# Two more pauses of the router with each scatter of rows to their slots

## The chip, the cores and the metric

The kernel runs on one core of a Trainium2 chip. The metric is the device time of one execution in microseconds: 3101.64 us in the median of three runs (3100.33 to 3101.95). TensorE does the matrix products, VectorE and ScalarE the arithmetic along rows, GpSimd causal selects, some arithmetic and indirect transfers, and SyncE issues most of the other transfers.

## The reference, cut to what matters

The model has two layers over x of shape 2 x 2048 x 256. The first layer normalises x and adds causal attention (16 heads of 16) and a mixture of experts:

```python
xn = _layernorm(x, axis=-1)
x = x + _L0_attn_ref(xn, ...) + _L0_ffn_ref(xn, ...)
```

In `_L0_ffn_ref` a second normalisation is followed by a gate: of eight experts (256 to 1024 to 256) each token takes the two with the largest logits, weighted by a softmax of the two. The second layer is a selective state space with a short convolution, and a ternary product beside it; nothing in this case touches it.

```python
logits = xn @ gate_w_moe + gate_b_moe
tw, ti = jax.lax.top_k(logits, K)
h = jax.nn.gelu(jnp.einsum('bsd,edf->besf', xn, w1) + b1[None, :, None, :], approximate=False)
```

The reference runs every expert on every token. The kernel sorts the tokens by expert instead, and that is where the change lies.

## The kernel before, in words

There are 4096 tokens, kept as 32 blocks of 128 rows. The kernel has four phases: a first one that normalises, projects q, k and v and computes the gate's logits; `attention`; `experts`; and `mix_and_state_space`. The first writes the normalised rows to DRAM (`n2_d`) and the parts of q and k too (`qk_d`).

Attention goes through 16 stages, each a batch and a pair of heads, numbered 0 to 15 here. Two generators work through them. `first` computes for every query the maximum over its keys (`maxima`, lines 652 to 678: scores on TensorE, reduced on VectorE). `second` follows 22 units behind (`LAG`) and does the attention proper (`attend`): scores again with the maximum subtracted (line 750), the exponential on ScalarE (line 758), and in the four key blocks that cross the diagonal of each group of 512 queries a causal select on GpSimd (line 763). A stage has 40 units in each generator; in `attend` they are four groups of 4, 8, 12 and 16 key blocks, whose last four each have a select, so a stage has 16 selects in groups of four. The value matmuls (line 705) wait for the exponential and, on the diagonal, for the select. They are put into the code some units later than their scores.

The q and k of a stage are loaded by `stacked` (line 554): 16 transfers of 128 KB on SyncE's queue, eight for q and eight for k. `first` calls it for stage s+1 when it begins stage s. There are three buffers for each, so the loads of stage 3 wait until stage 0's last scores are done, and so on.

Between these units the router runs (`route`). The loop in `attention` takes three units, then advances the router by one step, up to its next `yield`; there are 434 such steps. The router's first 25 steps compute on VectorE which experts each token takes and which slot (a row of `x_d` in DRAM) each of its two copies gets. Then, for block n of 32, it issues the load of block n+1 (`load`, line 973, on SyncE's queue, 128 KB) and two scatters (line 984): indirect transfers issued by GpSimd that write the block's 128 rows to their slots in `x_d`, once for each of the two experts. After each scatter it advances `finish_route`, which computes the experts' weights and row numbers, and yields; after the second there is one more yield. So a block takes three steps, and block n's first scatter is in step 26+3n. The tile `rows` has two buffers: row block n+2 can be loaded when both scatters of block n have landed. The scatters all write `x_d`, and each waits until the one before it has landed.

Attention is not in a manual schedule (that begins in the last phase). Tile lays down the order of each engine's queue when the program is built: an engine that is free takes, of the instructions whose inputs and buffers are held to be ready by then, the one that was written first. So instructions may be issued long before their place in the code when their engine is free. On the chip each queue runs in that fixed order.

`experts` reads `x_d` in tiles of 256 slots, after attention has ended.

Of the kernel before, what the change touches and what calls it, by code (L numbers as in the profile page):

```python
# [101 lines left out]
def tile_model(ctx: ExitStack, tc: tile.TileContext, t, out):  # L102
# [55 lines left out]
    with ExitStack() as c0:  # L158
# [9 lines left out]
        with tc.tile_pool(name="vs", bufs=1) as vsp, tc.tile_pool(name="qk", bufs=3) as qk:  # L168
# [6 lines left out]
            with tc.tile_pool(name="pa", bufs=2) as pa, tc.tile_pool(  # L175
# [154 lines left out]
                v,  # L330
                xa,
                lambda gp, ps: route(tc, row, ones, lg, n2_d, x_d, keep, stage, gp, ps, routes),
            )

# [515 lines left out]
def route(tc, row, ones, lg, n2_d, x_d, keep, stage, gp, ps_m, out):  # L850
# [120 lines left out]
    def load(n):  # L971
        rows = stage.tile([P, D], F32, tag="rows", name=f"rows_{n}")
        nc.sync.dma_start(rows, n2_d[:, n, :])
        coming.append(rows)
# [4 lines left out]
    for n in range(NT):  # L979
        if n + 1 < NT:  # L980
            load(n + 1)
        rows = coming.pop(0)
        for i in range(TOP):
            nc.gpsimd.indirect_dma_start(
                out=x_d[:, :],
                out_offset=bass.IndirectOffsetOnAxis(ap=slots[:, i, n : n + 1], axis=0),
                in_=rows,
                in_offset=None,
            )
            next(rest, None)  # L990
            yield
        next(rest, None)
        yield
    for _ in rest:
# [946 lines left out]
```

## Time and profile before

| | |
|---|---|
| median of three runs | 3101.64 us |
| the profiled execution | 3103.07 us |
| its span | 3101.4 us |
| granted TensorE clock, mean | 0.894 |
| the router's scatters | 238.4 to 539.1 us, 64 of them |
| attention's first causal select | 210.2 us |
| first load of an expert's weights | 1277.8 us |
| scatter, busy on GpSimd | 0.97 us in the median |
| scatter, issue to landing | 2.4 us in the median, 8.6 at most |

All durations come from one profiled execution, taken by the hardware profiler. An entry such as "PE pv L705 <- POOL p L763" reads: TensorE, about to run line 705, which writes the tile pv, stood idle until GpSimd had done line 763, which writes p. In the order of time a line gives the start and the length in us, the engine, the line of the code, the operation, and in brackets the idle time before it and what ended it; lines in a row of the same kind are merged with their count. SPq is SyncE's queue of transfers, and its lines show when transfers are issued, not when they land. The granted clock is a share of TensorE's full clock.

### The profile page before, as it was taken

The numbers are of one execution on the slowest core, as the hardware profiler recorded it, in microseconds if no ns is written. First come the engines' busy times: TensorE is split into PE (matmuls) and PEld (weight loads), VectorE is DVE, ScalarE is ACT, GpSimd is POOL, SyncE is SP. The second block draws the span as 40 slices with busy tenths as digits, with TensorE's granted clock in tenths as the row PEclk, the third lists the DMA queues.
The fourth block names the chain that finished last, engine by engine and source line by source line (L and its number), as shares of the span: only waits on it lengthen the run. The fifth ranks groups of instructions, "written<-read, shape, count | busy, mean of one in ns | idle before, by whom it ended". The sixth has DMA issues, their size and how long they took to land. (4 is left out here: it accounts for less than half of the span.)

```text
span 3101.4 us, 40083 instructions
## 1 busy us (share of the span) xinstructions
PE 2693.9 (87%) x15085; PEld 1472.6 (47%) x15085; DVE 2047.8 (66%) x2566; ACT 1577.7 (51%) x2522; POOL 1185.5 (38%) x933
## 2 busy tenths in 40 slices
PE   6887888999999999799999997687879889898867
PEld 4543433445444444587888886332323232332213
DVE  7576766887888888233111101368999898999996
ACT  3424555666566666422322222457666566666542
POOL 4313223000111011111112111267797887878775
PEclk9978988999999999899999999787888877788758
DMA  8843214112332210433445554124443634445350
GB/s 292 217 123 79 57 50 86 28 29 42 56 42 28 29 28 8 156 135 137 146 153 185 197 188 107 58 67 96 112 118 72 149 82 110 108 97 118 83 112 14
DMA packets 120086, 309.55 MB, mean 100 GB/s; under 512 B 27936, under 2 KB 70304, under 8 KB 102352
## 3 DMA queue, kind: packets, MB, share of 16 engines
q1 hardware_dynamic: 99968, 206.53, 28.2%
q0 software_dynamic: 18576, 99.24, 9.5%
q8 instruction: 122, 2.00, 0.3%
q10 hardware_dynamic: 1344, 1.16, 0.1%
q14 instruction: 76, 0.62, 0.1%
HBM read 228.48 MB, written 78.38 MB: 99 GB/s over the span
## 5 line engine op out<-in xcount | busy, mean ns | idle before, releaser
L758 ACT ACTIVATE p<-s 128x1024 f32<-128x1024 f32 (+3 forms) x640 | 563.3, 900 | 386.6 <-PE s L750 365.9
L665 DVE TENSOR_REDUCE best<-m 128x2 f32<-128x1024 f32 (+3 forms) x640 | 669.6, 1062 | 111.7 <-PE m L652 100.8
L1829 POOL TENSOR_TENSOR hh<-hh,cc 128x2048 f32<-128x2048 f32 x128 | 579.4, 4526 | 10.6 <-POOL carry L1828 0.4
L1817 DVE TENSOR_TENSOR_SCAN hh<-decay,uh 128x2048 f32<-128x2048 f32 x128 | 565.8, 4420 | 24.3 <-ACT decay L1703 10.5
L705 PE MATMUL pv<-p,v 128*17 128x256 f32 (+1 forms) x4608 | 384.2, 380 | 52.3 <-POOL p L763 49.5
L763 POOL TENSOR_SCALAR_AFFINE_SELECT p<-p 128x256 f32<-128x256 f32 x256 | 103.4, 408 | 787.0 <-ACT p L758 785.9
L1703 ACT ACTIVATE decay<-dd,a_neg 128x511 f32<-128x511 f32 x512 | 332.3, 711 | 54.7 <-DVE hh L1817 54.3
L1118 ACT ACTIVATE hT<-h,b1s 128x256 f32<-128x256 f32 x296 | 137.8, 473 | 385.9 <-PE h L1111 385.8
L1727 DVE TENSOR_TENSOR uh<-dd,bb 128x2048 f32<-128x2048 f32 x128 | 293.6, 2294 | 56.8 <-PE bb L1714 48.2
L1132 DVE TENSOR_TENSOR yt<-o,b 128x512 f32<-128x512 f32 x37 | 25.6, 691 | 436.8 <-PE o L1124 436.8
L750 PE MATMUL s<-q,k 64*128 64x512 f32 (+3 forms) x1280 | 287.9, 437 | 22.5 <-DVE best L665 17.5
L652 PE MATMUL m<-k,q 64*128 64x512 f32 (+3 forms) x1280 | 281.9, 427 | 18.0 <-DVE best L665 8.9
L1111 PE MATMUL h<-xT,w 128*128 128x256 f32 x1184 | 276.2, 387 | 19.9 <-ACT hT L1118 8.3
L1714 PE MATMUL bb<-xp_sb,w_dt 16*128 16x512 f32 x256 | 184.8, 808 | 103.8 <-DVE uh L1727 103.8
L1124 PE MATMUL o<-w,hT 128*128 128x256 f32 x1184 | 261.8, 379 | 0.0
L1074 POOL DMA_INDIRECT w<-in_w,wrow x74 | 71.2, 962 | 478.1 <-PE h L1111 255.3
L1111 PEld LDWEIGHTS h<-xT,w 128*128 128x128 f32 x1184 | 227.0, 194 | 55.0 <-ACT hT L1118 8.7
L750 PE MATMUL s<-tops,onesr 64*128 64x512 f32 (+3 forms) x1280 | 248.2, 371 | 0.0
L1124 PEld LDWEIGHTS o<-w,hT 128*128 128x128 f32 x1184 | 225.1, 190 | 30.5
L1744 PE MATMUL y<-hh,sel 128*32 128x512 f32 x1024 | 180.9, 787 | 57.5 <-POOL hh L1829 57.0
L705 PEld LDWEIGHTS pv<-p,v 128*17 128x17 f32 x4608 | 107.9, 97 | 235.5 <-issue 113.6
L750 PEld LDWEIGHTS s<-q,k 64*128 64x128 f32 x1280 | 127.0, 188 | 168.4 <-DVE best L665 55.8
(334 smaller groups left out, 3463.3 us busy)
## 6 DMA issues: line engine op xcount, KB each, us to landing
dd<-dd_d SPq DMA_DIRECT2D x120, 512.0 KB, 6.9
q<-qk_d SPq DMA_DIRECT2D x128, 128.0 KB, 4.1
k<-qk_d SPq DMA_DIRECT2D x128, 128.0 KB, 7.5
x_d<-zero SPq DMA_DIRECT2D x6, 1664.0 KB
xg<-x_d SPq DMA_DIRECT2D x37, 256.0 KB, 6.6
y_d<-yt SPq DMA_DIRECT2D x37, 256.0 KB, 2.2
qk_d<-qp SPq DMA_DIRECT2D x16, 512.0 KB, 3.7
qk_d<-kp SPq DMA_DIRECT2D x16, 512.0 KB, 3.3
```

The source lines that it names most:

```text
L652: nc.tensor.matmul(ps[:, h, 0:n], lhsT=qT[hs, qs], rhs=kT[hs, c * CH : c * CH + n], start=True, stop=True, tile_position=(HP * h, 0),)
L665: nc.vector.tensor_reduce(best[:, i, :, c], ps[:, :, 0:n], AX.X, ALU.max)
L705: nc.tensor.matmul(pv[r0 : r0 + HS + 1, lo - f * HC : HC], lhsT=v[:, b * TPB + kb, 2 * pr + h, :], rhs=pt[:, h, lo:hi], start=(kb == 0), s ...
L750: nc.tensor.matmul(ps[:, h, off:CH], lhsT=(kT[hs, kb * P : (kb + 1) * P], onesr[hs, :])[i], rhs=(qT[hs, j * CH + off : (j + 1) * CH], tp[h ...
L758: nc.scalar.activation(pt[:, :, off:CH], ps[:, :, off:CH], AF.Exp, scale=float(HS) ** -0.5)
L1111: nc.tensor.matmul(ph, lhsT=w1[:, k * DF + f * P : k * DF + (f + 1) * P], rhs=xT[:, k, :], start=(k == 0), stop=(k == 1),)
L1124: nc.tensor.matmul(po[:, h, :], lhsT=hT[:, f, h * P : (h + 1) * P], rhs=w2[:, f * D : (f + 1) * D], start=(f == 0), stop=(f == NF - 1),)
L1703: nc.scalar.activation(decay[G % 2][:, q, 1:], of[at]["dd", n // 4][:, 0, q, 1:], AF.Exp, scale=a_neg[:, q, n : n + 1],)
L1714: nc.tensor.matmul(bb[:, 0, :], lhsT=w_dt[DR + DS :, (n % 4) * P : (n % 4 + 1) * P], rhs=of[at]["xp"][DR + DS :, :], start=True, stop=True,)
L1727: nc.vector.tensor_tensor(uh, of[at]["dd", n // 4][:, 1], of[at]["bb", n].to_broadcast(full), ALU.mult)
L1817: nc.vector.tensor_tensor_scan(hh.rearrange("p q c -> p (q c)"), decay[G % 2].rearrange("p q c -> p (q c)"), uh.rearrange("p q c -> p (q c)"),
L1829: nc.gpsimd.tensor_tensor(hh, hh, m_["cc", g].to_broadcast(full), ALU.mult)
```

## The change

After each scatter, before the yield that was there, the router yields twice more.

```diff
                 in_offset=None,
             )
             next(rest, None)
+            yield
+            yield
             yield
         next(rest, None)
         yield
```

No instruction is added or removed. A block now takes seven of the router's steps instead of three: its first scatter is in step 26+7n, the second three steps later. The loads of the following blocks move along with it, and so do the first five advances of `finish_route`. The last scatter, which was in step 120, is in step 246 of 434.

## The prediction

> **What bounds the kernel now.** I read the page's engine totals first, then the busy time in stretches cut at attention's stages, then the list of waits between 230 and 560 us, where the scatters run, and last the order of time on SyncE's queue, on GpSimd and on TensorE around one of the long waits.
>
> ```profile
> PE 2693.9 (87%) x15085; PEld 1472.6 (47%) x15085; DVE 2047.8 (66%) x2566; ACT 1577.7 (51%) x2522; POOL 1185.5 (38%) x933
> ```
>
> TensorE is the busiest engine, but the share is an average. The change touches attention alone, so the next view is cut there: each line is one stage (a batch and a pair of heads), from its first causal select (line 763) to the next stage's. The last two numbers but one are the granted clock and the DMA share.
>
> ```profile
> 301.32:365.16 63.84, 59.77 (x526) 28.05 (x526) 48.07 (x80) 38.44 (x57) 15.21 (x25) 0.92 0.15 38
> 365.16:446.30 81.14, 63.71 (x555) 29.23 (x554) 54.76 (x91) 41.79 (x63) 20.05 (x30) 0.91 0.27 61
> 446.30:516.28 69.98, 63.10 (x540) 29.46 (x540) 50.89 (x81) 39.72 (x60) 23.01 (x33) 0.91 0.32 77
> 516.28:587.35 71.07, 58.82 (x526) 27.80 (x526) 50.01 (x83) 38.26 (x57) 11.27 (x22) 0.90 0.26 49
> 587.35:649.48 62.13, 59.41 (x545) 27.87 (x546) 52.01 (x85) 40.09 (x61) 6.46 (x17) 1.00 0.23 35
> 649.48:710.20 60.72, 58.73 (x546) 27.98 (x544) 52.01 (x85) 39.78 (x61) 6.45 (x16) 1.00 0.25 38
> ```
>
> These are stages 1 to 6. Stages 5 and 6 hold no scatter: TensorE is busy for 97% of them, and their mean, 61.4 us, is what a stage costs undisturbed. Stages 2, 3 and 4, with scatters, take 19.7, 8.6 and 9.7 us more. The waits say why; columns are us in total, times, longest:
>
> ```profile
> PE pv L705 <- POOL p L763: 49.0, 15, 10.9
> POOL x_d L984 <- DMA x_d<-rows,slots: 125.9, 53, 7.9
> ```
>
> A scatter may not start before the one before it has landed, and that wait stands in GpSimd's queue ahead of the causal selects; TensorE's value matmuls wait for the selects. One such place in full, start and length in us, GpSimd and then TensorE:
>
> ```profile
> 370.42 0.98 POOL L984 DMA_INDIRECT x_d<-rows,slots  x1 [1.80 <-DMA x_d<-rows,slots]
> 371.43 0.41 POOL L763 TENSOR_SCALAR_AFFINE_SELECT p<-p 128x256 f32<-128x256 f32 x1
> 373.39 0.99 POOL L984 DMA_INDIRECT x_d<-rows,slots  x1 [1.55 <-DMA x_d<-rows,slots]
> 378.49 0.97 POOL L984 DMA_INDIRECT x_d<-rows,slots  x1 [4.11 <-DMA x_d<-rows,slots]
> 387.17 0.97 POOL L984 DMA_INDIRECT x_d<-rows,slots  x1 [7.71 <-DMA x_d<-rows,slots]
> 389.86 0.97 POOL L984 DMA_INDIRECT x_d<-rows,slots  x1 [1.73 <-DMA x_d<-rows,slots]
> 390.85 1.12 POOL L763 TENSOR_SCALAR_AFFINE_SELECT p<-p 128x256 f32<-128x256 f32 x3
> 391.31 1.91 PE L705 MATMUL pv<-p,v 128*17 128x256 f32 x16 [10.91 <-POOL p L763]
> ```
>
> An undisturbed chain of scatters has one every 2.7 us (387.17 to 389.86). Here one takes 8.7 us, because a stage's sixteen q and k loads go out on SyncE's queue at that moment (a line with a count spans all its issues):
>
> ```profile
> 300.12 57.14 SPq L973 DMA_DIRECT2D rows<-n_d  x5
> 362.38 0.79 SPq L554 DMA_DIRECT2D q<-qk_d  x2
> 366.64 0.34 SPq L973 DMA_DIRECT2D rows<-n_d  x1
> 367.02 0.42 SPq L554 DMA_DIRECT2D q<-qk_d  x1
> 373.18 0.34 SPq L973 DMA_DIRECT2D rows<-n_d  x1
> 373.56 2.28 SPq L554 DMA_DIRECT2D q<-qk_d  x5
> 375.89 5.16 SPq L554 DMA_DIRECT2D k<-qk_d  x8
> 386.96 39.27 SPq L973 DMA_DIRECT2D rows<-n_d  x4
> ```
>
> The same happens four times. From the last uninterrupted run of q loads to the scatter that gets going again it is 12.4, 13.6, 12.9 and 13.8 us (287.92 to 300.31, 373.56 to 387.17, 467.73 to 480.60, 521.66 to 535.42), 13.2 in the mean.
>
> **What the change does to the order.** Two more yields add no instruction. They move each scatter, and the load issued with it, later in the code: block n goes from router step 26+3n to 26+7n, of 434 steps. The order on the engines does not simply follow: 19 scatters are issued by the end of stage 0 (301 us), where the code has reached 6, since GpSimd is idle and takes what is ready. The code's order decides only between things that are ready together, and it does so on SyncE's queue: the loads of stage 4's q and k are written at step 73. Rows 15 and 16 (steps 68, 71) are written before them and lie between them in the trace; row 17 (step 74) and later come after. With the change rows 8 and up are written after step 73, rows 12 and up after stage 5's loads (step 100), and so on. So from stage 4's loads on, each block of sixteen goes out undivided, and the rows wait behind it. Stage 3's loads show that form already: sixteen undivided, then five rows (300.12, the only gap of that kind) before stage 4's loads become ready. I therefore expect: nothing different up to about 362 us; then rows 15 to 19, 20 to 24, 25 to 29, 30 and 31 in the gaps behind the loads of stages 4, 5, 6 and 7, and the last scatter at about 620 us in place of 538 (three stages of 68 us after 365, and 38 us into the fourth, as in stage 1, plus four times 2.7).
>
> **The cost, part by part.** The issues themselves are the same 64 scatters of 0.97 us and 32 row loads; GpSimd is busy 6.5 of 61 us in a stage without scatters, so they lie beside other work, as 9 of them do in stage 1 (63.84 us, 2.4 over the plain 61.4, of which a wait of 1.5 after a collision is part). The later end costs nothing: x_d is read by the experts after 1277 us, some 650 us later. The rest of the router's arithmetic (finish_route) is issued at 223 us already, ahead of its place in the code, and is needed at 1277. A row load that now stands behind sixteen others delays only scatters, and in stage 1's form it is issued some 40 us before its scatter. So the cost lies in the collisions.
>
> At the loads of stage 4 the tail of the chain is rows 13 and 14 (scatters at 361.45, 364.15, 366.84, 370.42 in the trace). Undivided loads start where the first does now, 362.38, when stage 1's last scores free the buffer. 13.2 us on is 375.6, so the last scatter goes at 375.6 where it now goes at 370.42. The select behind it (371.43) and the value matmul behind that (371.89, which already waits 0.28 us for it) are late by 5.2 us. What follows a stall: stages 2, 3 and 4 lose 19.7+8.6+9.7 = 38.0 us, and their TensorE stalls of over 1.2 us sum to 28.3 (10.91, 2.37; 1.74, 1.65, 2.13; 1.22, 8.29): 9.7 us more over seven stalls, 1.4 each. So a boundary costs about 6.6 us. The bounds for it: 0, if the tail has passed, and 12.3, the largest stall plus 1.4. I take 6.6, since it is stage 4's own scatters that it is worked out from.
>
> After the change there are four such boundaries (into stages 2, 3, 4 and 5): 26.4 us. The other stalls of these stages (10.91, 8.29 and the small ones among divided loads) go. Before, stages 2 to 6 lose 19.7+8.6+9.7+0.7-0.7 = 38.0. The sum is -11.6 us. Against the profiled execution, 3103.07 us (span 3101.4 and 1.67 around it), that gives 3091.5; that execution lies 1.4 us over the median of the runs, so the median forecast is 3090.
>
> One rule speaks against a gain. The trace shows a lower granted clock after each stall: 0.73 in 310 to 320 us and 0.79 in 540 to 550, 1.00 in the stretches after. The Trainium skill, page "TensorE: Matmul & The Clock Gate", section Terms, prices throttled time at its length times one minus the clock ratio. The records show half clock in pieces of 3.4 to 13.7 us, mostly 6.8, so by that page a boundary is estimated at 5.2+3.4 = 8.6, four of them at 34.4, and the change at -3.6 us, within what can be measured. The trace disagrees in stage 4, where 9.5 us of stalls cost 9.7 us in all: a stage is not bound by the clock alone.
>
> **The rivals.** (1) Slower: the undivided loads cost the worst row at each boundary. Rows for it: 10.91 at 391.31, and 7.39 plus 1.53 at 301.79, where the loads were undivided too. Four times 12.3 is 49.2 against 38.0: +11, 3113. It decides from 9.5 us a boundary on. Against it: at 390 four scatters stood ahead of the select, and the new tail has one behind the last three selects. (2) The tail misses the loads: if only four rows fit into a gap, or the selects of the next stage come first, stages 3 to 5 cost some 0.7 each; 6.6+2.1 against 38.0 is -29, 3072. Against it: stage 1's gap held five. (3) The pauses do spread the scatters, one in three steps (61.4 us is 26.7 steps, so 6.9 us), longer than 2.7: every stall goes, also those of stage 0, where 62.9 us from the first scatter on hold 28 of 40 units of a stage, 43 us. That is 19.9+2.4+38.0 = -60, 3041. Against it: the 19 scatters in stage 0. (4) The order stays and nothing changes: 3101.6.
>
> **How the numbers follow.** Chances: forecast 0.42, (1) 0.28, (2) 0.13, (3) 0.08, (4) 0.09. Faster or slower begins at 0.2%, 6.2 us, about what a measurement of this kernel can tell from no change. Faster: 0.31 of the forecast, all of (2) and (3): 0.52. The same: 0.11 of the forecast, 0.05 of (1), 0.08 of (4): 0.24. Slower: 0.23 of (1) and 0.01 of (4): 0.24. The forecast's own range is 3080 to 3102. The whole range, 3064 to 3116, leaves out (3) and the far ends of (1) and (2).
>
> **What would show it.** Equal traces up to 362 us; sixteen undivided loads from about 362; five rows behind them; the last scatter near 620 us; TensorE waits of some 5 us at each of four boundaries; stages 2 to 5 at about 68 us and stage 6 at 61. Wrong would be: scatters 7 us apart from the start (rival 3), waits of 8 us or more at the boundaries (1), none (2), or a different stage 0.

## The result, and the profile after

The changed kernel takes 3116.84 us in the median of six runs (3115.22 to 3119.7), the kernel before 3098.47 us in the same comparison. The ratio is 1.0059, with a 95% interval from 1.0049 to 1.007: slower by 0.6%, where the forecast was faster by 0.4% (3090), and just above the end of its range (3116). The profiled execution after took 3118.85 us, with a span of 3117.1 against 3101.4, so 15.7 us more.

The first line of the page, engine totals with their shares and instruction counts, after:

```profile
PE 2707.8 (87%) x15085; PEld 1477.9 (47%) x15085; DVE 2048.8 (66%) x2566; ACT 1578.5 (51%) x2522; POOL 1185.6 (38%) x933
```

The work is the same and the times of VectorE, ScalarE and GpSimd agree within 1.0 us, but the same 15085 matmuls kept TensorE busy for 13.9 us longer (2693.9 before). So TensorE hardly waited longer: it worked more slowly. The stretches by stage say where; these are stages 1 to 6 after, each from its first causal select to the next stage's (the granted clock and the DMA share are the third- and second-last numbers):

```profile
302.83:363.83 61.00, 57.45 (x526) 27.21 (x527) 48.01 (x80) 38.42 (x57) 15.21 (x26) 0.96 0.17 40
363.83:444.60 80.77, 65.91 (x549) 30.05 (x548) 54.76 (x87) 41.41 (x62) 16.21 (x27) 0.87 0.31 57
444.60:519.50 74.90, 65.82 (x546) 30.57 (x546) 52.86 (x86) 40.47 (x61) 16.20 (x27) 0.89 0.26 55
519.50:591.02 71.52, 62.27 (x528) 28.92 (x528) 48.38 (x80) 38.26 (x57) 16.25 (x26) 0.84 0.26 52
591.02:664.00 72.98, 63.69 (x545) 29.13 (x546) 52.05 (x85) 40.29 (x61) 12.29 (x23) 0.91 0.26 46
664.00:724.69 60.69, 58.73 (x546) 27.98 (x544) 52.03 (x85) 39.78 (x61) 6.45 (x16) 1.00 0.26 37
```

Stages 2 to 6 take 360.86 us in sum and took 345.04 before: 15.8 more, which is the whole difference of the spans (what lies ahead of them is 1.3 us shorter, what follows 1.3 longer). Over the plain 61.4 us they lose 53.9 us, where the forecast had 26.4 and the kernel before 38.0. All of it lies in stages 2 to 5, which is where the forecast put its four boundaries.

SyncE's queue after (start, length from the first to the last issue, count):

```profile
361.04 3.62 SPq L554 DMA_DIRECT2D q<-qk_d  x8
364.70 7.03 SPq L554 DMA_DIRECT2D k<-qk_d  x8
372.48 66.29 SPq L973 DMA_DIRECT2D rows<-n_d  x5
```

From the loads of stage 4 on, sixteen q and k loads go out undivided with five rows behind them, as the prediction had it. The last scatter is at 648.56 us. So the order came out as forecast; what it costs did not. GpSimd and TensorE at the first of the four boundaries:

```profile
360.12 0.98 POOL L984 DMA_INDIRECT x_d<-rows,slots  x1 [0.32 <-issue]
362.82 0.98 POOL L984 DMA_INDIRECT x_d<-rows,slots  x1 [0.68 <-DMA x_d<-rows,slots]
370.10 0.98 POOL L984 DMA_INDIRECT x_d<-rows,slots  x1 [5.86 <-DMA x_d<-rows,slots]
371.11 0.77 POOL L763 TENSOR_SCALAR_AFFINE_SELECT p<-p 128x256 f32<-128x256 f32 x2
371.58 1.06 PE L705 MATMUL pv<-p,v 128*17 128x128 f32 x8 [4.58 <-POOL p L763]
379.08 0.98 POOL L984 DMA_INDIRECT x_d<-rows,slots  x1 [7.20 <-DMA x_d<-rows,slots]
380.09 0.41 POOL L763 TENSOR_SCALAR_AFFINE_SELECT p<-p 128x256 f32<-128x256 f32 x1
380.56 0.62 PE L705 MATMUL pv<-p,v 128*17 128x128 f32 x4 [4.24 <-POOL p L763]
```

The loads catch two scatters, not one: the one issued at 362.82 lands after 7.0 us and the next, at 370.10, after 8.7 (the scatters behind them go 7.3 and 9.0 us later, against 2.7 in an undisturbed chain). Each has a select behind it, and TensorE stalls twice, 4.58 and 4.24 us, with 4.7 us of work between. The last scatter of the tail goes 18.0 us after the first load (361.04 to 379.08). At the other three boundaries the stalls are 3.33 and 3.44 us; 3.79, 4.14 and 2.79; 3.48 and 3.58: in sum 33.4 us for four boundaries, 8.3 each.

Yet all waits of this kind together have hardly changed. The list of waits from 230 to 760 us (total, times, longest), after; before, the same entry was 49.0, 15 and 10.9:

```profile
PE pv L705 <- POOL p L763: 51.7, 17, 7.0
```

What changed is their lengths: five stalls of over 2.5 us before (3.60, 6.06, 7.39, 10.91, 8.29), twelve after, of which one is over 5. And with it the clock. Stretches around the first boundary after (length, TensorE's busy time, ..., granted clock, DMA share, GB/s):

```profile
367.00:371.60 4.60, 0.02 (x4) 0.02 (x5) 1.59 (x5) 0.38 (x1) 1.47 (x3) 0.69 1.01 155
371.60:376.30 4.70, 4.70 (x21) 1.46 (x21) 2.14 (x2) 2.05 (x5) 0.28 (x1) 0.50 1.00 127
376.30:380.60 4.30, 0.06 (x4) 0.05 (x4) 0.32 (x1) 0.00 (x0) 1.40 (x2) 0.50 0.53 95
380.60:389.40 8.80, 8.80 (x48) 4.24 (x50) 4.22 (x10) 3.44 (x4) 0.00 (x0) 0.51 0.10 30
389.40:398.00 8.60, 8.55 (x80) 4.05 (x72) 6.69 (x9) 4.49 (x6) 1.63 (x4) 1.00 0.00 0
```

and around the one long stall of the kernel before, at about the same place:

```profile
380.40:391.30 10.90, 0.01 (x2) 0.00 (x0) 1.68 (x2) 0.38 (x1) 2.39 (x4) 0.65 0.62 107
391.30:397.40 6.10, 6.08 (x36) 2.32 (x36) 1.66 (x2) 1.41 (x2) 1.07 (x3) 0.50 0.13 43
397.40:404.00 6.60, 6.32 (x61) 2.88 (x60) 5.32 (x9) 4.22 (x5) 0.00 (x0) 1.00 0.01 2
```

After, TensorE idles 8.8 us, and in between and afterwards works 13.5 us at half the clock. Before, it idles longer, 10.9 us, but only 6.1 us of work runs at half the clock: most of the slow clock falls into the stall itself, where there is nothing to slow down.

To add this up I cut 230 to 760 us of each kernel into stretches of one microsecond and summed TensorE's idle time, and the time that it worked at half the clock (where the clock changes within a stretch, the part at half clock, at most the busy time); the work in it takes twice its time, so half of it is lost.

| kernel | idle, us | working at half clock, us | idle + half of that | span |
|---|---|---|---|---|
| before | 65.8 | 47.5 | 89.5 | 3101.4 |
| after | 66.7 | 74.9 | 104.1 | 3117.1 |

The idle time accounts for 0.9 us of the difference and the clock for 13.7, together 14.6 of 15.7.

### The profile page after: what moved, and what is told of

It reads as the page before. It is cut to its first block, busy times and chain, and to the rows that moved or that the text cites. A ratio compares the mean times of both kernels' runs of the same rounds, so it can differ in the third digit from the quotient of the medians.

```text
span 3117.1 us, 40079 instructions
## 1 busy us (share of the span) xinstructions
PE 2707.8 (87%) x15085; PEld 1477.9 (47%) x15085; DVE 2048.8 (66%) x2566; ACT 1578.5 (51%) x2522; POOL 1185.6 (38%) x933
## 5 line engine op out<-in xcount | busy, mean ns | idle before, releaser
L1819 DVE TENSOR_TENSOR_SCAN hh<-decay,uh 128x2048 f32<-128x2048 f32 x128 | 565.8, 4420 | 24.4 <-ACT decay L1705 10.5
L652 PE MATMUL m<-k,q 64*128 64x512 f32 (+3 forms) x1280 | 284.3, 430 | 17.1 <-DVE best L665 8.6
```

What stands on the lines that cost most here:

```text
L652: nc.tensor.matmul(ps[:, h, 0:n], lhsT=qT[hs, qs], rhs=kT[hs, c * CH : c * CH + n], start=True, stop=True, tile_position=(HP * h, 0),)
L1819: nc.vector.tensor_tensor_scan(hh.rearrange("p q c -> p (q c)"), decay[G % 2].rearrange("p q c -> p (q c)"), uh.rearrange("p q c -> p (q c)"),
```

## The experiments

The theory, from this reading: the loss lies where a chain of scatters, each waiting for the one before, is still unfinished when the next stage's loads go out; the landings then take 7 to 9 us instead of 2.4 and the selects behind them are late. Rivals: the loads alone cost it, whatever the scatters do; the divided order of before is cheap in itself; the scatters cost by their number. The first five kernels are variants of the changed kernel and are compared with the kernel before by their times; the last three are variants of the fourth and are read from their profiles.

**No chain at the later boundaries.** Row loads and scatters of blocks 15 to 31 are left out, so those rows of `x_d` are not written.

```diff
-    for n in range(NT):
-        if n + 1 < NT:
+    for n in range(15):
+        if n + 1 < 15:
```

> The changed kernel without the row loads and scatters of blocks 15 to 31, so that x_d lacks them; all else is kept, and the queues' order is the changed kernel's up to the boundary into stage 2. Theory (the loss sits at the boundaries, where undivided q and k loads hold up the tail of the scatters): stage 2 keeps the first boundary's two stalls, 4.6 and 4.2 us, and takes about 75 us, stages 3, 4 and 5 fall from 74.9, 71.5 and 73.0 to about 61.4, and the time to about 3076. Rival (the undivided loads disturb TensorE by themselves, scatters or not, by traffic or by the clock): stages 3 to 5 stay above 68 and the time above 3100.

It took 3073.41 us, 0.9903 of before (0.9884 to 0.9922). Stages 2 to 4:

```profile
364.27:439.18 74.91, 64.65 (x545) 29.80 (x546) 52.23 (x85) 40.30 (x61) 8.39 (x18) 0.89 0.21 34
439.18:499.89 60.71, 58.74 (x546) 27.96 (x544) 52.07 (x85) 39.88 (x61) 6.51 (x17) 1.00 0.25 37
499.89:559.42 59.53, 56.93 (x536) 27.08 (x534) 51.12 (x85) 39.81 (x60) 6.51 (x16) 1.00 0.27 36
```

Without scatters the undivided loads of the following stages cost nothing: 60.7 and 59.5 us at full clock. The one boundary that is left still has its two stalls, 4.42 us (ending at 371.88) and 3.64 (380.26), and stage 2 takes 74.9 us, 13.5 over the plain 61.4. Stage times and total came out as the theory had them (about 75, about 61.4, about 3076).

**No loads.** From stage 4 on the buffers of earlier stages are used again, so the q and k of stages 4 to 15 are wrong and 192 loads are missing.

```diff
-                    stacks[s + 1] = stacked(nc, qk, qk_d, s + 1)
+                    stacks[s + 1] = stacks[s - 2] if s > 2 else stacked(nc, qk, qk_d, s + 1)
```

> The changed kernel without the q and k loads of stages 4 to 15, which compute with the tiles of three stages before. Nothing then holds the row loads back, so the scatters run on through stages 1 to 3, still each waiting for the landing before it. Theory: without the loads no scatter waits more than about 3 us once stage 3's loads are done, TensorE's stalls in stages 2 and 3 stay under 2.5 us each, these stages cost 3 to 6 us over 61.4, stages 4 and 5 nothing, and the time is about 3070 to 3080. Rival (each stage with scatters costs some 10 to 13 us, loads or not): stages 2 and 3 stay above 71 and the time is about 3085 to 3095.

3081.27 us, 0.994 of before (0.9923 to 0.9957). The time was near what was expected, but not the picture. The order moved with it: all scatters were issued by 461.88 us, 29 of them in stage 2, which took 82.6 us:

```profile
360.63:443.21 82.58, 65.43 (x555) 29.81 (x554) 54.28 (x88) 41.51 (x63) 34.68 (x46) 0.90 0.21 70
```

It had stalls of 1.71, 4.61, 1.66 and 5.38 us, without any q or k load beside it (row loads go on). The chain at its undisturbed 2.7 us per scatter is enough to make selects late where many scatters stand in a row. So the loads are a part of the cause, not the whole.

**Rows ahead of q and k.** The row loads are given priority on SyncE, so that they divide the loads as before the change and more.

```diff
-        nc.sync.dma_start(rows, n2_d[:, n, :])
+        with tc.high_priority():
+            nc.sync.dma_start(rows, n2_d[:, n, :])
```

> The changed kernel, pauses and all, with the row loads alone put first in the order (high priority), so that they lie between the q and k loads even more than in the kernel before; the scatters keep their pauses in the code. Theory (the pauses act only through the order of row loads against q and k loads): the pauses then do nothing, the scatters run ahead and end in stage 2, q and k loads are spread out, and a scatter costs about 0.5 us as in stage 3 of the kernel before (8.6 us for 17): some 22 us for the 44 after stage 0, against 40 in the kernel before, and a time of about 3080. Rival (it is the scatters' own place that costs): the time stays near the changed kernel's, above 3105.

A miss: 3105.76 us, 1.0019 of before (1.0009 to 1.003), where about 3080 was expected. The time is the rival's (above 3105), its reason is not: the last scatter goes at 447.03, so the scatters did move ahead. But stages 1 and 2 take 93.1 and 81.9 us, with stalls up to 11.23 us:

```profile
296.05:389.14 93.09, 61.64 (x524) 28.88 (x524) 49.84 (x82) 38.44 (x58) 33.72 (x45) 0.82 0.29 83
389.14:471.08 81.94, 65.13 (x548) 29.90 (x548) 52.48 (x85) 40.31 (x61) 22.88 (x33) 0.87 0.28 70
```

Divided loads are little cheaper; the same chain stalls elsewhere.

**No waits between scatters.** Their rows are different slots, so no scatter needs the one before; they are declared independent. Nothing else is changed, and nothing left out.

```diff
+    apart = []
...
-            nc.gpsimd.indirect_dma_start(
+            inst = nc.gpsimd.indirect_dma_start(
...
-            )
+            ).ins
+            for earlier in apart:
+                tc.declare_no_dep(inst, earlier, reason="their rows are different slots")
+            apart.append(inst)
```

> The changed kernel in which a scatter no longer waits for the landing of earlier scatters: the program declares that the scatters do not depend on each other, since no two rows share a slot. The q and k loads and all scatters stay, and the loads go out undivided. Theory (it is the wait for a landing, standing in GpSimd's queue ahead of the selects, that stalls TensorE): the stalls of 3 to 5 us at the boundaries go, stages 1 to 5 take 61 to 64 us, and the time falls to 3045 to 3060, some 57 to 72 less; what is left is waits for row loads in stage 0. Rival (the traffic, the clock or GpSimd's work on scatters costs by itself): disturbed stages stay near 70 and the time above 3085.

3063.14 us, 0.9878 of before (0.9862 to 0.9895), a little above the expected range. The order changes too: 34 scatters go in stage 0, against 19, and the last goes at 426.43. So the run shows what the waits cost together with the order that Tile builds around them; no run takes the waits away and keeps the order. Stages 1 to 3:

```profile
299.15:364.43 65.28, 59.09 (x548) 27.99 (x546) 53.49 (x87) 41.35 (x63) 22.10 (x33) 1.00 0.32 76
364.43:427.43 63.00, 58.68 (x536) 27.00 (x536) 50.91 (x83) 39.01 (x60) 20.05 (x31) 1.00 0.36 78
427.43:488.09 60.66, 58.28 (x542) 27.75 (x540) 51.36 (x84) 39.58 (x60) 6.51 (x17) 1.00 0.25 40
```

The clock is 1.00 from stage 1 on, though GpSimd issues 16 and 14 scatters in stages 1 and 2 (33 and 31 instructions against 17). What is left are stalls of 3.41, 8.46 and 2.69 us in stage 0, where scatters wait for their rows (two buffers).

**Half of the waits.** Only the second scatter of a block is declared independent of the first; the first still waits for the block before. The edit is shown against the kernel without waits.

```diff
-            for earlier in apart:
+            for earlier in apart[-1:] if i else ():
```

> The changed kernel, where of the two scatters of one block the second no longer waits for the first (the first still waits for the block before). The order of TensorE's, GpSimd's and SyncE's work is close to that of the kernel with no waits between scatters (twenty scatters in stages 0 and 1 each, ten or so at a time ahead of loads), and half of the waits are left. If the cost is that of the serial chain of landings, halving the waits leaves about half of what taking all of them away saved (3117 - 3063 = 54): 3085, 3075 to 3095, with stalls of 2 to 5 us at one scatter of a pair only. If instead only a scatter caught behind the stage's q and k loads costs anything, one scatter a boundary is still caught and waits as long as before: near 3100. If scatters cost by their number whatever they wait for, it stays at 3110 or above.

3060.47 us, 0.9863 of before (0.9842 to 0.9885): not half of the saving but all of it. GpSimd's chain in it, around 340 us:

```profile
339.08 0.97 POOL L985 DMA_INDIRECT x_d<-rows,slots  x1 [2.67 <-DMA rows<-n_d]
340.36 0.97 POOL L985 DMA_INDIRECT x_d<-rows,slots  x1 [0.30 <-issue]
341.64 0.97 POOL L985 DMA_INDIRECT x_d<-rows,slots  x1 [0.30 <-issue]
343.04 0.97 POOL L985 DMA_INDIRECT x_d<-rows,slots  x1 [0.43 <-DMA x_d<-rows,slots]
345.73 0.96 POOL L985 DMA_INDIRECT x_d<-rows,slots  x1 [1.72 <-DMA rows<-n_d]
```

The longest waits are for rows now; a block's two scatters take the 2.7 us of one. At the end of stage 1 the last two scatters of the tail go at 355.85 and 357.14, while the first loads go out at 356.30, so none of them waits on a landing that the loads delay. The landings are slow here too, 5.7 us for the scatter at 357.14 and 9.5 for the one at 422.31 at the end of stage 2, but no select waits behind them, and the next scatter is due much later. So it is not the slow landing that costs, but the wait for it. I read this as a threshold: a chain that is through before the next select and the next loads costs little, whatever it waits inside. It is read from one kernel, whose order moved too (34 scatters in stage 0 here as well). The expectation, which took the cost to be proportional to the waits, was wrong.

**The price of one stall.** Stages 8 to 15 of the kernel without waits are undisturbed, and in this kernel and the two after it stage 7, which is left alone, agrees with it (70.78, 70.78 and 70.77 us against 70.82). In four of them one select is made late: it waits for a transfer that copies w columns of its input element by element to DRAM, where nothing reads them. TensorE's order shifts by a few instructions at these places.

```diff
                         dg = pt[:, :, off : off + P]
+                        w = {8: 8, 10: 16, 12: 32, 14: 64}.get(s, 0)
+                        if w and (j, kb) == (3, 12):
+                            nc.sync.dma_start(out=late_d[:, 0:w, 0], in_=dg[:, 0, 0:w])
```

> The kernel with no waits between scatters (3063), whose stages 8 to 15 are undisturbed, with one artificial lateness in each of stages 8, 10, 12 and 14: the select of the thirteenth key block of the last query chunk waits for a transfer of 8, 16, 32 and 64 columns of its probabilities to DRAM, element by element (nothing reads them; the output is the same). It measures what one stall of TensorE costs by its length, in stages that nothing else disturbs, by stage time, stall and time at the half clock. If a stall costs itself and a fixed 1.4 us, as the prediction had it, a stage with a 4 us stall is 5.4 us longer than the same stage without. If the half clock that follows it costs a third of its length beside, a 4 us stall with 7 to 10 us at half clock costs 6.5 to 7.5 us.

The four waits on TensorE, in stages 8, 10, 12 and 14:

```profile
803.58 1.05 PE L707 MATMUL pv<-p,v 128*17 128x256 f32 x8 [3.87 <-POOL p L768]
935.98 1.91 PE L707 MATMUL pv<-p,v 128*17 128x256 f32 x16 [9.97 <-POOL p L768]
1086.72 1.05 PE L707 MATMUL pv<-p,v 128*17 128x256 f32 x8 [26.19 <-POOL p L768]
1253.47 1.05 PE L707 MATMUL pv<-p,v 128*17 128x256 f32 x8 [41.86 <-POOL p L768]
```

and the same four stages, in stretches:

```profile
736.15:808.95 72.80, 65.68 (x571) 32.48 (x572) 53.53 (x87) 41.10 (x63) 6.45 (x16) 0.95 0.27 40
869.57:940.94 71.37, 58.76 (x534) 27.86 (x532) 51.05 (x84) 39.82 (x60) 6.51 (x16) 0.90 0.36 40
1003.44:1092.69 89.25, 60.35 (x546) 28.48 (x544) 52.22 (x85) 39.89 (x61) 6.46 (x16) 0.85 0.32 28
1152.23:1258.97 106.74, 61.77 (x546) 28.64 (x546) 52.46 (x85) 40.10 (x61) 6.46 (x16) 0.79 0.43 1
```

Without the lateness these stages take 66.31, 59.54, 60.67 and 62.16 us. They lose 6.5, 11.8, 28.6 and 44.6 us: the stall and 2.6, 1.9, 2.4 and 2.7 beside it. The surcharge hardly depends on the stall's length here, since the half clock lasts on for 3.8 to 4.5 us after the end of each of the four, and half of that is lost. Idle time beyond that of the undisturbed stage and half of the work at half clock add up to 6.1, 12.3, 28.9 and 44.5 us, each within 0.5 of the loss. By this price a wait of a given total costs more in many pieces than in one, and a 4 us stall costs 6.5, where the prediction had 5.4.

**Two stalls, close together and apart.** Lateness of one kind, 12 columns, in stages 9 to 14.

```diff
+                        first = {9: (2, 8), 10: (2, 8), 11: (1, 4), 12: (2, 8), 13: (2, 8), 14: (1, 4)}
+                        second = {10: (2, 11), 11: (3, 12), 13: (2, 11), 14: (3, 12)}
+                        if (j, kb) in (first.get(s), second.get(s)):
+                            nc.sync.dma_start(out=late_d[:, 0:12, 0], in_=dg[:, 0, 0:12])
```

> The kernel with no waits between scatters, with artificial lateness in its undisturbed stages: a select waits for a transfer of 12 columns of its probabilities to DRAM, element by element (nothing reads them). Stages 9 and 12 have one such stall (first diagonal block of the third query chunk); stages 10 and 13 have two close together, some 10 us apart (first and last diagonal block of the third chunk), as the changed kernel has at each boundary; stages 11 and 14 have two some 40 us apart. The ladder of single stalls gave 1.8 to 2.7 us beside each stall's own length. If stalls close together cost more than their number, stages 10 and 13 lose well over twice the surcharge of stages 9 and 12 (over 7 us beside the stalls, with one stretch of about 20 us at half clock), and stages 11 and 14 lose twice (4 to 5 us, two stretches of 7). If it is their number that counts, 10, 11, 13 and 14 are alike, 4 to 5.5 us beside the stalls' length.

Stages 9 and 12 lost 6.4 and 6.9 us, 10 and 13 (close together) 9.5 and 9.2, 11 and 14 (apart) 13.1 and 18.2. This does not settle it, because the stalls were not alike: value matmuls were issued later at (2, 8), so that the single stall dissolved into small gaps (the longest 1.40 us), and those far apart were 2.64 and 4.81, and 5.80 and 5.38 us, with 5.7 and 7.0 us lost beside them, more than was expected. It gives no sign that neighbours are dearer, and it shows a loss of 6.4 us, with 10.2 us at half clock, where TensorE never idled for more than 1.4 us in one piece (stage 9).

**Two stalls close together, as a sum.** 20 columns at (2, 8) in stages 9, 10, 12 and 13; 12 columns at (2, 11) in stages 10, 11, 13 and 14.

```diff
+                        early = 20 if s in (9, 10, 12, 13) and (j, kb) == (2, 8) else 0
+                        late = 12 if s in (10, 11, 13, 14) and (j, kb) == (2, 11) else 0
+                        w = early or late
+                        if w:
+                            nc.sync.dma_start(out=late_d[:, 0:w, 0], in_=dg[:, 0, 0:w])
```

> The same artificial lateness in undisturbed stages, to see whether two stalls some 10 us apart cost the sum of the two: in stages 9 and 12 only the select of the third chunk's first diagonal block is late (a transfer of 20 columns), in stages 11 and 14 only that of its last diagonal block (12 columns), in stages 10 and 13 both. By TensorE's idle time and half of the time that it works at the half clock, each stage's loss should come out within 1 us. If stalls close together cost more than apart, stages 10 and 13 lose at least 3 us more than the sum of the two single ones, in one stretch of 17 to 20 us at half clock; if not, the three agree within 1.5 us, and the changed kernel's longer stretches come from elsewhere.

Stages 9 to 11, the early one alone, both, and the late one alone:

```profile
803.58:874.81 71.23, 62.20 (x546) 29.59 (x544) 51.72 (x85) 40.10 (x61) 6.50 (x17) 0.90 0.25 32
874.81:951.48 76.67, 60.62 (x536) 28.08 (x534) 51.03 (x85) 40.04 (x60) 6.50 (x17) 0.87 0.22 28
951.48:1020.00 68.52, 62.49 (x546) 28.64 (x546) 52.05 (x85) 39.97 (x61) 6.45 (x16) 0.95 0.24 32
```

Undisturbed they take 60.68, 59.54 and 62.15 us, so they lose 10.5, 17.1 and 6.4: both cost the sum of the two (16.9). In stages 12 to 14 it is 13.1, 18.0 and 8.0, so both cost 3.1 less than the sum. The time at half clock behaves alike: 20.5 us in stage 10 against 13.7 and 6.8 for the two alone, 20.5 in stage 13 against 17.1 and 6.8. So nothing here makes two late selects dearer for being close together. The pieces were again not quite alike: the late one alone made no gap of over 1.32 us in stage 11, where in stage 10 it stalled TensorE for 4.39, and the early one alone stalled it for 3.99, with the other for 6.81. What does hold in every one of the six stages is the sum of extra idle time and half of the work at half clock: 11.1, 17.4, 6.1, 13.4, 19.0 and 8.5 us, within 1.0 of the losses.

The same sum as for before and after, idle time and half of the work at half clock from 230 to 760 us, for the kernels with all stages intact:

| kernel | idle, us | working at half clock, us | sum, against before | span, against before |
|---|---|---|---|---|
| changed | 66.7 | 74.9 | +14.6 | +15.7 |
| rows ahead | 68.1 | 45.9 | +1.5 | +2.6 |
| no waits | 39.9 | 13.1 | -43.1 | -39.9 |
| half of the waits | 34.7 | 18.1 | -45.8 | -43.4 |

The two terms explain the spans within some 3 us. Rows ahead and the changed kernel idle about as long; what lies between them is mostly the clock.

## Why the prediction was wrong

*What bounds the kernel* stood: the serial chain of scatters makes the selects late, and taking its waits away (declared independent) saves 53.7 us against the changed kernel, as much as stages 2 to 6 lose in it. *The order* came out as forecast: sixteen undivided loads from 361 us (forecast 362), rows 15 to 19 behind them and so on, the same four boundaries. Ahead of them SyncE's order is that of before; stage 0 takes 91.27 us against 91.17, and stage 1 61.00 against 63.84. The last scatter was at 648.56 us and not 620, mostly because the stages in between were longer. *The issues cost nothing* nearly stood: in the kernel without waits, 16 and 14 scatters in stages 1 and 2 leave the clock at 1.00, and these stages take 3.9 and 1.6 us over the plain 61.4.

What failed is the cost of one boundary, 6.6 us where stages 2 to 5 lost 53.9 in all with stage 6's -0.7, so 13.5 each. Both of its terms were too small.

The first is the stall of 5.2 us; measured, 8.3. I took the tail of before's chain, left all of it but the last scatter where it was, and moved that one. But the loads catch two scatters, which hold the next one back by 7.3 and 9.0 us, so the last one goes 18.0 us after the first load and not 13.2, and there are two stalls a boundary, once three. The 13.2 was a mean over four places of before, three of them with divided loads and counted from the last uninterrupted run of q loads; at the one with undivided loads, into stage 3, I stopped at the first scatter that got going (300.31) and not at the last:

```profile
287.92 3.60 SPq L554 DMA_DIRECT2D q<-qk_d  x8
300.31 0.99 POOL L984 DMA_INDIRECT x_d<-rows,slots  x1 [7.27 <-DMA x_d<-rows,slots]
305.92 0.99 POOL L984 DMA_INDIRECT x_d<-rows,slots  x1 [3.84 <-DMA x_d<-rows,slots]
```

That is 18.0 us from the first load to the last scatter as well, with two stalls, 7.39 and 1.53: the row that I used for rival 1 alone was the nearest one.

The second is what follows the stalls of a boundary, 1.4 us; measured, 5.2 (13.5 less 8.3). It was taken once, where a boundary has two or three stalls, and it was too small for each: nine stalls at four boundaries lose 20.5 us beside their length, 2.3 each. The 1.4 was a mean over seven stalls of which two were long and four under 2.2 us. The ladder of single stalls shows 1.9 to 2.7 us a stall, at lengths from 4 to 42 us; two of 4 to 7 us in one stage gave more still (17.1 us lost for 11.2 of stalls and a gap of 1.4).

Against before the same holds in one line: the change left the idle time where it was (65.8 to 66.7 us) and cut it into more pieces, and the work at half clock rose from 47.5 to 74.9 us. The 10.91 and 8.29 us stalls, which the forecast rightly had removed, were the cheap kind for their length.

I had weighed the rule of the Trainium skill, "TensorE: Matmul & The Clock Gate", section Terms, that throttled time costs its length times one minus the clock ratio, and set it aside with the words that the trace disagrees. The runs agree with it, if the throttled time is counted where TensorE works: 27.4 us more of it, times one half, is 13.7 us, of 15.7 measured. The objection that stage 4 lost no more than its stalls came from the plain 61.4: without scatters stage 4 takes 59.5 us (499.89:559.42 above), so before lost 11.5 us there for 9.5 of stalls. The rule's reading at the time, 8.6 us a boundary, was short in both terms: the stalls were 8.3 us and not 5.2, and TensorE worked at half clock for some 13.6 us a stage in stages 2 to 5, where the estimate had one piece of 6.8 us.

Of the rivals, the first was nearest in time, 3113 at 12.3 us a boundary, past its point of 9.5. Its mechanism was not what happened: there is no stall of 11 us but two of 4, and the clock. Its price was drawn from the largest stall, so its time came near by luck. The second and third did not occur, and the order did change (the fourth).

Not settled is what sets the time at half clock after a given stall: 6.8 to 17.1 us in these runs for single stalls of 3.9 to 7.0 us (two of them with a gap of 1.4 ahead), and 6.8 to 10.2 us where small gaps alone add up. The single stalls of the last experiment lost from 1.5 us (6.48 in stage 14) to about 5 beside their idle pieces, so the ladder's price is not a fixed one.

## What to carry to other kernels

A chain of transfers in which each waits for the last to land cost little here where it was through before the next thing behind it, and much where it was not: count whether it is through before the next thing behind it on its queue is due, with the landing time that the trace shows under the heaviest traffic, and count how many links that traffic catches. If the links write different places, say so to the scheduler; halving the waits was enough here and gave 1.4% (0.9863). And where TensorE is nearly always busy, price a stall by its length and, for each stall, the work that then runs at the lower clock; equal idle time in more pieces is dearer.

## What the runs showed of the hardware

- A scatter that lands in 2.4 us alone took 7.0 and 8.7 us when a stage's sixteen loads of 128 KB were under way, with the DMA engines' share at 1.0 for most of the time.
- In the ladder a stall of TensorE cost 1.9 to 2.7 us beside its length, from 3.87 to 41.86 us; TensorE went back to the full clock 3.8 to 4.5 us after the end of each. Single stalls elsewhere cost 1.5 to about 5 us.
- The granted clock fell to half for 10.2 us without any idle piece of over 1.4 us: in the 10.2 us before, TensorE had been busy for 8.51.
- Transfers of single elements make a fine-grained delay: 128 rows of 8 to 64 columns held a select back so that TensorE stalled for 3.87 to 41.86 us.
